# Order of the first and fourth unit, and the engine of some copies, in a two-layer transformer kernel

## The chip, the cores and the metric

The kernel runs on one core of a Trainium2 chip. A core has a matrix engine (TensorE, PE in the profile), a vector engine (VectorE, DVE), a scalar engine (ScalarE, ACT), a general engine (GpSimd, POOL) and SyncE (SP), which here only issues DMA transfers. Each engine works through its own queue in order and waits at semaphores for the others. Matmul results land in PSUM, everything else is in SBUF. The metric is the device time of one execution in microseconds (us); before the change the median of three runs is 738.88 us (738.88 to 739.01).

## The reference

The input `x` has four sequences (b) of 256 rows and 256 columns. Two layers follow each other, each an attention and a feed-forward part, each added to `x` after a layer norm. All is float32.

```python
def attn0(x):                              # 16 query heads, 8 key/value heads of 128
    q = einsum('btd,ndh->btnh', x, q_kernel); k, v = einsum('bsd,ckdh->cbskh', x, kv_kernel)
    q = apply_rope(rms_norm(q, q_norm_scale)); k = apply_rope(rms_norm(k, k_norm_scale))
    p = softmax(where((j <= i) & (i - j < 128), q @ k.T * 0.0884, -big))
    return einsum('btnh,nhd->btd', p @ v, out_kernel)
def ffn0(x):                               # keeps the 2 largest of each 4 columns of h
    h = silu(x @ w_gate) * (x @ w_up)
    return sparsify_2to4(h) @ w_down
def attn1(x):                              # 16 heads, causal, no rotation
    return softmax(causal(x @ W_Q @ (x @ W_K).T) * 0.0884) @ (x @ W_V) @ W_O
def ffn1(x):                               # fwht: Walsh-Hadamard transform of 1024 columns
    return fwht(silu(x @ W1.T) * (x @ W3.T)) @ W2.T
x = x + attn0(norm(x)); x = x + ffn0(norm(x)); x = x + attn1(norm(x)); x = x + ffn1(norm(x))
```

The lines are shortened: heads are written as matrix products. `rms_norm` divides each head's row by the root of its mean square; `apply_rope` turns its first and second half against each other by an angle that grows with the row.

## The kernel before

**Units.** Each attention is cut into 16 units. In attention 0 unit `n` is sequence `b` and head group `g` with `b, g = divmod(n, 4)`: 4 query heads and 2 key/value heads. A sequence's 256 rows are two blocks `t` of 128. Units go through a pipeline of stages (`pipelined`, lines 299 to 311): in step `s` stage `k` works on unit `s - lags[k]`, and the stages of one step are written in the sequence `order`. `behind` holds work that is written after a step.

**Stages of attention 0.** `project` (line 329, `project0`) multiplies the normed rows by the weights of 4 query heads, and by those of 2 keys and 2 values, block by block (matmul at line 443 into a bank `pj`). VectorE multiplies each result by a cosine and a sine table (line 448, `qc` and `qs`), ScalarE squares it (line 453, `sq`) and copies the values (line 455). `rotate` (`rotate0`, line 458) adds `qc` to `qs` with its halves exchanged (line 466, 768 columns: 6 heads), sums the squares of each head (line 467, `ss`), and on GpSimd makes the factors `r`, one over a root (lines 480, 483 and the power at 486, for 12 columns at once), with which it scales the keys (line 489). `turn` (`turn0`, line 495) transposes queries and keys: for units 0 to 5 and 14, 15 on TensorE (lines 504 and 515), with copies out of PSUM by VectorE (505) and ScalarE (516); for the rest the queries go over GpSimd (475) and a transposing DMA (477). `score` (`probabilities`, line 201) has score matmuls (213, 214), VectorE's masked maxima (216) and `nb` (223), ScalarE's exponentials (226), the reciprocal `rs` (231, VectorE) and GpSimd's scaling by it (234). `split` (`planes`, line 242) sorts each probability's two 16-bit halves apart on GpSimd (240) and sends them through a transposing DMA (249). `join` (`joined`, line 252) puts the turned halves together again (260), in attention 0 by ScalarE for both heads of a pair `kk`. `attend` multiplies with the values (391, 395). `out` multiplies by the output weights (292).

**Banks.** The results `pj` and the turned queries of the TensorE path share four PSUM slots (`half`); scores, turned keys of the TensorE path and `av` share four others (`bank`). A tile that gets a slot waits until the tile four before it has been read.

**Attention 1** has the same plan with stages `project`, `score` and `attend` (lines 691 to 726); products are formed by seven block products in place of eight (`seven_products`), whose last sums and copies are known as `last_of["sum"]` and `last_of["copy"]`. Its `joined` gives the first head of each pair to ScalarE and the second to VectorE.

**What sets the order.** The sequence within an engine's queue is made when the program is built, by a planner that takes the instructions in the order written but lets a later one pass where, by its modelled costs, an earlier one isn't ready. `tc.issue_after(x)` keeps the instructions of a block behind `x` on `x`'s engine. In the trace, for instance, unit 0's sum of block 0 (line 466) stands at 13.48 us, before the key products of block 1 (line 448) at 14.36. SyncE's transfers are issued as written: x of sequence 0, the identity, `wq` group 0, the tables, `wkv` group 0, x of sequence 1, then the rest.

Of the kernel before, what the change touches and what calls it, by code (L numbers as in the profile page):

```python
# [48 lines left out]
def two_layers(ctx, tc, consts, tables, x, wq, wkv, wo, w_gate, w_up, w_down,  # L49
# [49 lines left out]
    def attn_weight(name):  # L99
        return apool.tile([P, 4, NC, 512], F32, name=name)  # L100

    def load_group(t, src, g):
        nc.sync.dma_start(t[:, g], src[:, g])
# [8 lines left out]
    load_x(0)  # L112
    nc.sync.dma_start(cst[:, C_ID:C_HAD], consts[:, C_ID:C_HAD])
    wq_sb, wkv_sb = attn_weight("wq"), attn_weight("wkv")
    load_group(wq_sb, wq, 0)
    nc.sync.dma_start(tab, tables)
    load_group(wkv_sb, wkv, 0)
    load_x(1)
    nc.sync.dma_start(cst[:, C_HAD:], consts[:, C_HAD:])
    for g in range(1, 4):  # L120
# [193 lines left out]
    def attention0():  # L314
        with tc.tile_pool(name="attn0", bufs=2, reuse_waits="tile", side="right") as own:
# [22 lines left out]

            def rotated(n, held):
                rot, v = held  # L340
                rot, qT_planes, r = rotate0(rot, n >= 6, last_of["mx"] if 2 <= n < 14 else None)
                return rot, qT_planes, v, r

            def rotate(n, held):
                return rotated(n, held) if n < 14 else held

            def turn(n, held):
                rot, qT_planes, v, r = held
# [20 lines left out]
            def join(n, held):  # L369
                ps, v = held  # L370
                return [
                    joined(ps[kk], ((nc.scalar.copy, slice(0, 2), last_of["exp"]),))
                    for kk in range(2)
                ], v

# [26 lines left out]
            def out(b, t, gs, kept=False):  # L402
# [15 lines left out]
            behind[17] = [lambda _: xn_f.append(normed(0))]  # L418
            behind[19] = [lambda _: xn_f.append(normed(1)), *(out(3, t, (2, 3)) for t in range(NT))]
            pipelined(  # L420
                (project, rotate, turn, score, split, join, attend), (0, 0, 1, 2, 3, 4, 4),
                behind, (0, 5, 4, 3, 1, 2, 6),
            )

    def project0(own, xnT, g, cos_s, sin_s, first):


        v = own.tile([P, NT, 2, HD], F32, tag="v", name="v", bufs=5)
        rot = [
            [own.tile([P, 6, HD], F32, tag=tag, name=tag, bufs=n)  # L430
             for tag, n in (("qc", 4), ("qs", 2), ("sq", 2))] for _ in range(NT)
        ]

        queries, rest = (wq_sb, slice(0, 4)), (wkv_sb, slice(4, 6))
        parts = [(t, *part) for t in range(NT) for part in (queries, rest)]
        if first:
            parts = [(t, *part) for part in (queries, rest) for t in range(NT)]
        for t, w, hs in parts:
            qc, qs, sq = rot[t]
            pj = half([4, HD], "pj")  # L440
            n = hs.stop - hs.start
            for c in range(NC):
                last_of[0] = nc.tensor.matmul(  # L443
                    pj, lhsT=xnT[:, c, t * P : (t + 1) * P], rhs=w[:, g, c, :],
                    start=(c == 0), stop=(c == NC - 1),
                )
            for rot_to, tab in ((qs, sin_s), (qc, cos_s)):
                last_of["qc"] = nc.vector.tensor_tensor(  # L448
                    rot_to[:, hs], pj[:, 0:n],
                    tab[:, t, hs.start // 4, :].unsqueeze(1).to_broadcast([P, n, HD]),  # L450
                    ALU.mult,
                )
            nc.scalar.activation(sq[:, hs], pj[:, 0:n], AF.Square)  # L453
            if n == 2:
                last_of["v", t] = nc.scalar.copy(v[:, t, :, :], pj[:, 2:4])
        return rot, v

    def rotate0(rot, by_dma, first):

        r = small.tile([P, NT, 6], F32, tag="r", name="r")  # L460
        ss = small.tile([P, NT, 6], F32, tag="ss", name="ss")
        for t, (qc, qs, sq) in enumerate(rot):

            parts = [i.rearrange("p n (s h) -> p n s h", s=2) for i in (qc, qs)]
            with tc.issue_after(first.ins) if first else nullcontext():
                nc.vector.tensor_tensor(parts[0], parts[0], parts[1][:, :, ::-1, :], ALU.add)
            nc.vector.tensor_reduce(ss[:, t, :], sq, AX.X, ALU.add)
            rot[t] = qc
        qT_planes = None
        if by_dma:  # L470

            planes = page_of_planes([P, NT, 2, 4 * HD], "qpl")
            for t, qc in enumerate(rot):
# [1 line left out]
                copy_gpsimd(planes[:, t], words.rearrange("p (n w) -> p w n", w=2))  # L475
            qT_planes = page_of_planes([P, NT * 2 * 4, P], "qplT")
            nc.sync.dma_start_transpose(qT_planes, planes.rearrange("p t w n -> p (t w n)"))

        ve = small.tile([P, NT, 6], F32, tag="ve", name="ve")
        nc.gpsimd.tensor_scalar(  # L480
            ve[:, :, 0:4], ss[:, :, 0:4], 1.0, HD * RMS_EPS, ALU.mult, ALU.add
        )
        nc.gpsimd.tensor_scalar(
            ve[:, :, 4:6], ss[:, :, 4:6], 1.0 / HD, RMS_EPS, ALU.mult, ALU.add
        )
        nc.gpsimd.tensor_tensor(r.rearrange("p t h -> p (t h)"), ve.rearrange("p t h -> p (t h)"),
                                mhalf, ALU.pow)
        for t, qc in enumerate(rot):
            last_of["k"] = nc.gpsimd.tensor_tensor(
                qc[:, 4:6, :], qc[:, 4:6, :],  # L490
                r[:, t, 4:6].unsqueeze(2).to_broadcast([P, 2, HD]), ALU.mult,
            )
        return rot, qT_planes, r

    def turn0(own, rot, qT_planes, bank_of_k):
# [192 lines left out]
    def attention1(finish_ffn0):  # L688
# [23 lines left out]
        def attend(n, held):  # L712
# [3 lines left out]
            zTs[n] = zT = page("zT1")  # L716
            for kk in range(2):
                pT = joined(ps[kk], (
                    (nc.scalar.copy, slice(0, 1), last_of["copy"]),
                    (nc.vector.tensor_copy, slice(1, 2), last_of["sum"]),  # L720
                ))
                av = bank([2, T], "av1")
# [269 lines left out]
```

## Time and profile before

| | |
|---|---|
| Median of 3 runs | 738.88 us |
| The profiled execution | 737.64 us |
| Its span | 735.9 us |
| TensorE busy | 725.6 us (99%) |
| VectorE busy | 465.2 us (63%) |
| ScalarE busy | 412.2 us (56%) |
| GpSimd busy | 347.9 us (47%) |
| Granted TensorE clock | 1.00 in the span |

The profile is of one execution; its span runs from the first to the last instruction of the core, and what lies around the span makes up the rest of its time. Engine rows are shares of the span. "PEld" is TensorE's loading of weights, which overlaps its matmuls. Each float32 matmul of the program stands in the trace as two instructions. Attention 0 lasts to about 270 us, the first feed-forward part to about 375, attention 1 to about 645, the second feed-forward part to the end; they overlap at their seams.

### The profile page before, as it was taken

The numbers are of one execution on the slowest core, as the hardware profiler recorded it, in microseconds if no ns is written. First come the engines' busy times: TensorE is split into PE (matmuls) and PEld (weight loads), VectorE is DVE, ScalarE is ACT, GpSimd is POOL, SyncE is SP. The second block draws the span as 40 slices with busy tenths as digits, with TensorE's granted clock in tenths as the row PEclk, the third lists the DMA queues.
The fourth block names the chain that finished last, engine by engine and source line by source line (L and its number), as shares of the span: only waits on it lengthen the run. The fifth ranks groups of instructions, "written<-read, shape, count | busy, mean of one in ns | idle before, by whom it ended". The sixth has DMA issues, their size and how long they took to land.

```text
span 735.9 us, 11600 instructions
## 1 busy us (share of the span) xinstructions
PE 725.6 (99%) x3912; PEld 595.1 (81%) x3912; DVE 465.2 (63%) x1398; ACT 412.2 (56%) x987; POOL 347.9 (47%) x489
## 2 busy tenths in 40 slices
PE   9999999999999999999999999999999999999998
PEld 5556576666666778888898999999998999899997
DVE  6999878888887517977655644464442755464443
ACT  2487887667767962322356555555556576434332
POOL 1588978897799821011125433343336575520000
PEclk9999999999999999999999999999999999999999
DMA  8732354425446444001224432342232223401100
GB/s 333 289 65 53 56 93 81 92 52 94 89 76 101 86 121 166 16 14 45 99 72 86 126 48 44 77 124 44 44 73 44 44 44 44 91 12 22 24 13 30
DMA packets 138348, 57.51 MB, mean 78 GB/s; under 512 B 131504, under 2 KB 133680, under 8 KB 137520
## 3 DMA queue, kind: packets, MB, share of 16 engines
q1 hardware_dynamic: 138288, 56.77, 33.7%
q8 instruction: 31, 0.51, 0.3%
q14 instruction: 29, 0.24, 0.1%
HBM read 22.94 MB, written 1.05 MB: 33 GB/s over the span
## 4 chain that ended last, share of the span: by engine, by line
PE 73%; DVE 9%; POOL 7%; ACT 4%; issue 4%; DMA 2%; SPq 0%; POOLq 0%; ACTq 0%; DVEq 0%
PE pj L443 10%; PE pgu L547 8%; PE po_f L592 7%; PE po L292 7%; PE qk_x L777 5%; PE po L280 5%; PE sc L214 5%; PE gu_x L852 4%; PE av L391 3%; PE qk_y L777 3%; PE v_x L783 3%; PE av L268 2%; PE sc L213 2%; POOL p L234 2%; PE gu_y L852 2%
## 5 line engine op out<-in xcount | busy, mean ns | idle before, releaser
L234 POOL TENSOR_SCALAR p<-p,rs 128x128 f32<-128x128 f32 (+1 forms) x256 | 114.2, 464 | 149.9 <-DVE rs L231 144.6
L240 POOL TENSOR_SCALAR pl<-p 128x1536 uint16<-128x1536 uint16 x64 | 96.6, 1510 | 4.3
L260 ACT COPY pT<-plT 128x1536 uint16<-128x1536 uint16 (+1 forms) x64 | 92.0, 1493 | 11.6 <-DMA plT<-pl 11.6
L216 DVE CUSTOM_DVE_ANT_0 p<-sc,cst 128x128 f32<-128x128 f32 (+1 forms) x256 | 79.8, 352 | 10.4 <-PE sc L214 7.8
L226 ACT ACTIVATE p<-p,nb,r 128x128 f32<-128x128 f32 (+1 forms) x128 | 68.2, 534 | 18.8 <-DVE nb L223 18.7
L443 PE MATMUL pj<-wq,xnT 128*128 128x512 f32 x128 | 61.1, 595 | 1.1 <-DVE qT L505 1.1
L443 PE MATMUL pj<-wkv,xnT 128*128 128x512 f32 x128 | 60.1, 592 | 0.0
L292 PE MATMUL po<-wo,zT 128*128 128x256 f32 x256 | 57.9, 379 | 0.0
L226 ACT ACTIVATE p<-p,nb 128x128 f32<-128x128 f32 (+1 forms) x128 | 56.3, 447 | 2.8 <-DVE nb L221 2.8
L280 PE MATMUL po<-w_o,zT 128*128 128x256 f32 x256 | 57.6, 379 | 0.0
L453 ACT ACTIVATE sq<-pj 128x512 f32<-128x512 f32 (+1 forms) x64 | 31.0, 491 | 42.6 <-DVE qc L448 42.2
L292 PEld LDWEIGHTS po<-wo,zT 128*128 128x128 f32 x256 | 48.3, 190 | 7.0 <-ACT kT L516 0.6
L280 PEld LDWEIGHTS po<-w_o,zT 128*128 128x128 f32 x256 | 47.7, 190 | 6.0
L156 POOL TENSOR_SCALAR ve<-mv 128x2 f32<-128x2 f32 (+1 forms) x17 | 3.7, 220 | 98.1 <-DVE mv L152 97.6
L443 PEld LDWEIGHTS pj<-wkv,xnT 128*128 128x128 f32 x128 | 24.3, 190 | 30.2 <-issue 28.5
L448 DVE TENSOR_TENSOR qs<-pj,sin_s 128x512 f32<-128x512 f32 (+1 forms) x64 | 35.3, 552 | 13.4 <-PE pj L443 12.9
L443 PEld LDWEIGHTS pj<-wq,xnT 128*128 128x128 f32 x128 | 23.5, 190 | 24.2 <-issue 20.1
L663 ACT COPY qk<-qk_x 128x512 f32<-128x512 f32 x16 | 9.4, 587 | 57.6 <-PE qk_x L777 53.0
L268 PE MATMUL av<-pT,v 128*128 128x256 f32 x128 | 38.5, 383 | 1.0 <-ACT pT L260 0.9
L214 PE MATMUL sc<-kT,qT 128*128 128x256 f32 x128 | 38.3, 381 | 0.0
L214 PE MATMUL sc<-qk 128*128 128x256 f32 x128 | 38.2, 380 | 0.0
L240 POOL TENSOR_SCALAR qpl<-qc 128x1024 uint16<-128x1024 uint16 x20 | 29.2, 1474 | 18.0 <-PE av L395 8.2
(151 smaller groups left out, 1747.8 us busy)
## 6 DMA issues: line engine op xcount, KB each, us to landing
w<-in_w_dram SPq DMA_DIRECT2D x3, 1024.0 KB, 4.7
wq<-in_wq_dram SPq DMA_DIRECT2D x4, 512.0 KB, 7.6
wkv<-in_wkv_dram SPq DMA_DIRECT2D x4, 512.0 KB, 8.2
wo<-in_wo_dram SPq DMA_DIRECT2D x4, 512.0 KB, 10.2
w_qk<-in_w_q_dram SPq DMA_DIRECT2D x4, 512.0 KB, 4.8
w_qk<-in_w_k_dram SPq DMA_DIRECT2D x4, 512.0 KB, 5.8
w_v<-in_w_v_dram SPq DMA_DIRECT2D x4, 512.0 KB, 7.1
w_o<-in_w_o_dram SPq DMA_DIRECT2D x4, 512.0 KB, 6.1
```

The source lines that it names most:

```text
L214: nc.tensor.matmul(sc[:, P : 3 * P], lhsT=q[:, P:T], rhs=k, start=True, stop=True)
L216: last_of["mx"] = nc.vector.tensor_tensor_reduce(out=p[:, j, cols], in0=sc[:, cols], in1=mask[:, cols], scale=1.0, scalar=-3.0e38, op0=ALU ...
L226: last_of["exp"] = nc.scalar.activation(p[:, j, cols], p[:, j, cols], AF.Exp, bias=nb[:, j, i : i + 1], scale=SCALE1 if rq is None else rq ...
L234: nc.gpsimd.tensor_scalar(p[:, j, cols], p[:, j, cols], rs[:, j, i : i + 1], 1.0, ALU.mult, ALU.mult)
L240: last_of["planes"] = nc.gpsimd.tensor_scalar(o, i, 1.0, 1.0, ALU.mult, ALU.mult)
L260: copy(words.rearrange("p (n w) -> p w n", w=2), halves[:, :, js].rearrange("p w j n -> p w (j n)"),)
L268: nc.tensor.matmul(av, lhsT=v0, rhs=pT[:, 0:T], start=True, stop=False, skip_group_check=True)
L280: nc.tensor.matmul(po[:, t, :], lhsT=zT[:, j, t * P : (t + 1) * P], rhs=w[:, j, :], start=(t == j == 0), stop=(j == 3), skip_group_check=True,
L292: nc.tensor.matmul(po, lhsT=zTs[hd // 4][:, hd % 4, t * P : (t + 1) * P], rhs=w[:, hd, :], start=(hd == 0), stop=(hd == n - 1),)
L443: last_of[0] = nc.tensor.matmul(pj, lhsT=xnT[:, c, t * P : (t + 1) * P], rhs=w[:, g, c, :], start=(c == 0), stop=(c == NC - 1),)
L547: nc.tensor.matmul(o[:, j, :], lhsT=w[:, c, f0 + j, :], rhs=xnT[:, c, :], start=(c == 0), stop=(c == NC - 1),)
L777: last_of[1] = nc.tensor.matmul(o[:, j, :], lhsT=wqk[i - 1][:, j // 2, j % 2, :], rhs=x[i - 1], start=(first and j == 0), stop=True, skip_ ...
```

## The change

There are four edits.

1. The transfers of `wkv` group 0 and `wq` group 0 swap places. Unit 0 projects keys and values of both blocks first and then the queries of both. Its rotation is done apart: sums, squares' sums and factors of the two keys first, their scaling, and then the same for the four queries. Powers are taken per block there (two of 2 columns and two of 4) in place of one of 12. For the other units the same instructions are issued as before, now from the helpers `factors0` and `scaled`.
2. The rotation of unit 3 moves from the stage before `turn` of unit 2 in that step to a new stage `rotate_late` right behind it.
3. In attention 0 VectorE, not ScalarE, joins the second pair (`kk == 1`) of units 14 and 15.
4. In attention 1 VectorE, not ScalarE, joins the first head of both pairs of unit 0, without the constraint to stand behind a product's copy; the second head was VectorE's already.

```diff
     wq_sb, wkv_sb = attn_weight("wq"), attn_weight("wkv")
+    load_group(wkv_sb, wkv, 0)
+    nc.sync.dma_start(tab, tables)
     load_group(wq_sb, wq, 0)
-    nc.sync.dma_start(tab, tables)
-    load_group(wkv_sb, wkv, 0)
     load_x(1)
...
             def rotate(n, held):
-                return rotated(n, held) if n < 14 else held
+                return rotated(n, held) if n != 3 and n < 14 else held
+
+            def rotate_late(n, held):
+                return rotated(n, held) if n == 3 else held
...
                 return [
-                    joined(ps[kk], ((nc.scalar.copy, slice(0, 2), last_of["exp"]),))
+                    joined(ps[kk], ((
+                        nc.vector.tensor_copy if kk == 1 and n >= 14 else nc.scalar.copy,
+                        slice(0, 2), last_of["exp"],
+                    ),))
                     for kk in range(2)
...
             pipelined(
-                (project, rotate, turn, score, split, join, attend), (0, 0, 1, 2, 3, 4, 4),
-                behind, (0, 5, 4, 3, 1, 2, 6),
+                (project, rotate, turn, rotate_late, score, split, join, attend),
+                (0, 0, 1, 0, 2, 3, 4, 4),
+                behind, (0, 6, 5, 4, 1, 2, 3, 7),
             )
...
         if first:
-            parts = [(t, *part) for part in (queries, rest) for t in range(NT)]
+            parts = [(t, *part) for part in (rest, queries) for t in range(NT)]
...
+    def factors0(r, ss, ve, hs):
+        for part, scale, eps in ((slice(0, 4), 1.0, HD * RMS_EPS), (slice(4, 6), 1.0 / HD, RMS_EPS)):
+            if hs.start <= part.start < hs.stop:
+                nc.gpsimd.tensor_scalar(
+                    ve[:, :, part], ss[:, :, part], scale, eps, ALU.mult, ALU.add
+                )
+        o, i = (
+            [a[:, t, hs] for t in range(NT)] if hs.stop - hs.start < 6 else
+            [a.rearrange("p t h -> p (t h)")] for a in (r, ve)
+        )
+        for o_t, i_t in zip(o, i):
+            nc.gpsimd.tensor_tensor(o_t, i_t, mhalf[:, 0 : o_t.shape[-1]], ALU.pow)
...
-    def rotate0(rot, by_dma, first):
+    def rotate0(rot, by_dma, first, apart):
...
+        for hs in (slice(4, 6), slice(0, 4)) if apart else (slice(0, 6),):
+            for t, (qc, qs, sq) in enumerate(rot):
+                parts = [i[:, hs].rearrange("p n (s h) -> p n s h", s=2) for i in (qc, qs)]
+                with tc.issue_after(first.ins) if first else nullcontext():
+                    nc.vector.tensor_tensor(
+                        parts[0], parts[0], parts[1][:, :, ::-1, :], ALU.add
+                    )
+                nc.vector.tensor_reduce(ss[:, t, hs], sq[:, hs], AX.X, ALU.add)
+            if apart:
+                factors0(r, ss, ve, hs)
+                if hs.start == 4:
+                    scaled([qc for qc, _, _ in rot], r)
...
+        if not apart:
+            factors0(r, ss, ve, slice(0, 6))
+            scaled(rot, r)
         return rot, qT_planes, r
...
                 pT = joined(ps[kk], (
-                    (nc.scalar.copy, slice(0, 1), last_of["copy"]),
+                    (
+                        (nc.vector.tensor_copy, slice(0, 1), None) if n < 1 else
+                        (nc.scalar.copy, slice(0, 1), last_of["copy"])
+                    ),
                     (nc.vector.tensor_copy, slice(1, 2), last_of["sum"]),
                 ))
```

## The prediction

> **What bounds the kernel now.** I read the page's busy row first, then TensorE's waits, then the timelines around the places where it waits. The page says:
>
> ```profile
> span 735.9 us, 11600 instructions
> PE 725.6 (99%) x3912; PEld 595.1 (81%) x3912; DVE 465.2 (63%) x1398; ACT 412.2 (56%) x987; POOL 347.9 (47%) x489
> ```
>
> TensorE works nearly all the time, and the change leaves its matmuls as they are. So all that can be won is idle time of TensorE: 735.9 - 725.6 = 10.3 us, with 1.2 us before its first matmul and about 3 us after its last. The list of its waits (total, times, longest) names who ends them:
>
> ```profile
> PE tr_k L515 <- POOL qc L489: 1.6, 2, 1.2
> PE pj L443 <- DVE qT L505: 1.1, 2, 0.9
> PE av L391 <- DVE mx L216: 1.0, 2, 0.8
> PE av L268 <- ACT pT L260: 0.9, 2, 0.7
> ```
>
> The timeline of TensorE places them (start, duration, and in brackets the idle time before):
>
> ```profile
> 22.14 0.44 PE L515 MATMUL tr_k<-cst,qc 128*128 128x128 f32 x2 [1.22 <-POOL qc L489]
> ...
> 50.09 1.98 PE L443 MATMUL pj<-wq,xnT 128*128 128x512 f32 x4 [0.91 <-DVE qT L505]
> ...
> 72.05 1.13 PE L391 MATMUL av<-pT,v 128*128 128x512 f32 x2 [0.83 <-DVE mx L216]
> ...
> 399.02 0.70 PE L268 MATMUL av<-pT,v 128*128 128x256 f32 x2 [0.68 <-ACT pT L260]
> ```
>
> Matmul ends are modelled, so I count from start to start: a 128x128 matmul normally gives way to the next after 0.22 us with its pair, and by that count the four places cost about 1.38, 1.07, 0.99 and 0.84 us. The first two and the last are where three of the edits work. But the share of VectorE by stretch shows a second bound at the beginning:
>
> ```profile
> core 0: us, PE busy (x) PEld busy (x) DVE busy (x) ACT busy (x) POOL busy (x), PEclk, DMA share, GB/s
> 30.00:40.00 10.00, 9.80 (x46) 6.28 (x45) 9.86 (x33) 6.52 (x22) 6.05 (x9) 1.00 0.13 53
> 40.00:50.00 10.00, 9.17 (x41) 5.70 (x39) 9.90 (x32) 7.65 (x25) 6.86 (x11) 1.00 0.43 79
> 60.00:70.00 10.00, 10.00 (x37) 5.87 (x37) 9.93 (x26) 9.02 (x20) 8.99 (x14) 1.00 0.42 78
> 90.00:100.00 10.00, 10.00 (x35) 6.07 (x34) 6.10 (x12) 7.77 (x16) 8.93 (x14) 1.00 0.51 94
> ```
>
> VectorE is full from 10 to about 72 us and has room only after 78. Between 10 and 72 us a hole closed in TensorE is worth only what VectorE then finishes sooner, since the wait at 72.05 is for VectorE's maxima. VectorE's own idle time there is small:
>
> ```profile
> 28.42 0.69 DVE L448 TENSOR_TENSOR qs<-pj,sin_s 128x512 f32<-128x512 f32 x1 [0.45 <-PE pj L443]
> 30.14 0.42 DVE L448 TENSOR_TENSOR qs<-pj,sin_s 128x256 f32<-128x256 f32 x1 [0.43 <-PE pj L443]
> ```
>
> From 100 to 230 us TensorE goes through its units at 15.96 us each with GpSimd idle 2 us in most, so what is ahead at 78 us stays ahead.
>
> **The change, part by part.**
>
> *First unit's keys first and apart.* The two weight loads swap places on SyncE's queue; both are 512 KB, landing at 5.99 and 9.05 us, and the part projected first needs its weights at 6.49, the second at 10.02. Either order fits: 0. The tables and both x loads keep their places behind the same bytes. The keys' products are then with VectorE from 10.3 us on, and their sums can end between 13.0 us (right behind the four 0.33 us products) and about 15.5 us (behind the queries' products too). GpSimd then needs one 0.20 us factor step, two powers of two columns (0.70 us each by the L157 row of that size) and two scalings at 0.61: 2.9 us with issue, so keys stand at 16 to 19 us, before TensorE turns them at 20.8. The queries' two powers of four columns, by interpolation between 0.70 us (2 columns) and 2.27 (12), are 1.0 us each; they end by 21.5, and nobody needs them before the first `nb` at 34.58. So the hole of 1.38 closes. What is late next: two projection banks of unit 2 wait for the copies of the turned queries (VectorE, 24.83), and VectorE is full. It gains its two pauses, 0.53 + 0.50 = 1.03 us from start to start, and pays for splitting two sums and two reductions: 768 columns take 0.86 us from start to start, 256 take 0.33 and 512 take 0.60, so 0.93 - 0.86 = 0.07, four times: 0.28. The scalings now fall near VectorE's own L466 sums. A collision costs VectorE from 0 to two times 0.61; I take 0.2. Part: -1.03 + 0.28 + 0.2 = -0.55, rounded **-0.6**.
>
> *Fourth unit's sums behind the third's turn.* The two copies (1.2 us) pass ahead of two sums and two reductions (3.5 us), so the bank of the matmul at 50.09 comes free before it is wanted at 49.0: 1.07 us closes. But VectorE has the same work, and reaches unit 4's products at 50.5 as before. It saves only pauses behind TensorE near 53.8 and 55.9, with their rounding about 0.35. Behind TensorE's gained time the next wait is the fourth unit's keys: L489 began at 56.08 and `tr_k` at 56.74 already followed on its heels, after GpSimd had worked without a pause since 47.68. That start hangs on `rs` (L231, 47.42) in VectorE's queue between the very sums that move. It moves by -0.4 to +3.0 us. TensorE stood 0.83 us at 72.05, which is its spare for this. I take no effect of it, and 0.35 from VectorE: **-0.35**.
>
> *Who meets whom.* In this stretch VectorE lost time to GpSimd:
>
> ```profile
> 57.53 1.98 DVE L466 TENSOR_TENSOR qc<-qc,qs 128x768 f32<-128x768 f32 x1
> 57.23 1.47 POOL L240 TENSOR_SCALAR pl<-p 128x1536 uint16<-128x1536 uint16 x1
> 70.60 1.06 DVE L223 SCALAR_TENSOR_TENSOR nb<-mx,r 128x4 f32<-128x4 f32 x1
> 70.17 1.47 POOL L240 TENSOR_SCALAR pl<-p 128x1536 uint16<-128x1536 uint16 x1
> ```
>
> The sum takes 0.95 and `nb` 0.16 elsewhere; both ended here just behind the GpSimd copy. With those at 44.03 and 56.11 such losses are 3.1 us. The edits shift the two engines against each other, so they are dealt anew: at best TensorE's whole 0.93 at 72.05 goes, at worst it grows by as much. I take 0, and +-0.9 for the range.
>
> *VectorE at the end of attention 0* (second pair of units 14 and 15). TensorE has no hole there: 253 to 362 us is solid, with `av` of unit 15's second pair issued at 268.73 and ScalarE's copy done at 268.2. VectorE's copy would take about 1.0 us (a 128x1024 one takes 0.68, a 128x768 one 0.59) in place of 1.92, but it starts with the transfer's landing, and it may push GpSimd's work at 258.3 by up to 1.0. The holes at 250.8 and 252.7 belong to unit 13, which the edit leaves alone: **0**. Were that cover gone, ScalarE's 0.95 would be its worth.
>
> *VectorE at the start of attention 1* (unit 0, first head of each pair). For the second pair ScalarE copies at 397.93, behind four exponentials; the data landed at 394.30. On VectorE, idle from 396.64 to 398.06, the copy ends at 397.2; TensorE would ask at 398.18. The 0.84 hole closes. For the first pair it is open. ScalarE finished at 395.60 and TensorE lost 0.31 there. The data landed at 391.14, but VectorE's queue was full to 395.49. The row of these copies is 0.59 us, and if one fits in before 393 the 0.31 goes too, with 0.1 of restart: -1.25. The Trainium skill speaks against that: "SBUF — State Buffer", section "Who interferes with whom", says that a VectorE copy in a two-port mode and a GpSimd instruction exclude each other, and whichever comes second waits for the first to end. GpSimd's L240 runs from 393.62 to 395.09, so a copy put there would end no earlier than 395.6, and with both heads in one queue at 396.0: +0.4, so -0.44 for the part. This trace has both kinds: one copy at 592 ns beside no GpSimd work, another at 1053 under it. I take the middle, **-0.85**. The maxima behind such a copy feed unit 1's exponentials up to 1 us later; its pair is joined at 406.6 and later, having landed at 405.18, so with some cover.
>
> Sum: -0.6 - 0.35 + 0 + 0 - 0.85 = **-1.8 us**. The profiled execution took 737.64 (span 735.9 and 1.7 around it): 735.8 expected. The runs' median is 738.88, 1.2 above it, and I carry the difference over: **737.1**.
>
> **The rivals.**
> - *Both seams and the collisions too.* The new phase frees 0.93 at 72.05, and the first pair's copy fits early (-0.4 more): -1.8 - 1.3 = -3.1, 735.8. For it: the losses are chance meetings of 0.6 to 1.5 us instructions. Against: GpSimd is 90% busy from 60 us on, so others wait.
> - *VectorE keeps the early gain.* The start gives nothing because VectorE is full and has four more instructions; only attention 1 pays: 738.0 to 738.4. For it: 9.9 of 10 us busy. Against: the two pauses at 28 and 30 us.
> - *Slower: `rs` gets behind all the sums.* If the planner sets unit 1's `rs` behind two copies and four sums, it comes at 45.7 + 1.2 + 3.5 = 50.4 in place of 47.42. GpSimd's unbroken run to L489 starts 3.0 later, unit 3's keys come 3.0 later, TensorE has 0.83 of spare: +2.2, and with the later meetings of GpSimd and VectorE at worst +3.1. Less 0.6 of the first part and 0.85 at attention 1: +1.65, 740.5. Without such meetings it passes 0.2% (1.48 us) only from 1.48 + 0.6 + 0.85 + 0.83 = 3.8 us of lateness, with the worst of them from 2.9. Against: `rs` stood between the sums before.
>
> **How the numbers follow.** Main case 0.46 (own range 736.3 to 737.9), collisions freed 0.20, early gain kept by VectorE 0.21, slower 0.13. What a measurement can tell from no change is about 0.2%, 1.48 us: the line is 737.4. The main case lies on its fast side for two thirds (0.31), so faster 0.31 + 0.20 = 0.51; same 0.15 + 0.21 = 0.36; slower 0.13. The range goes down to 735.3 (the second case's edge) and up to 739.9, which takes in the slower case's beginning and leaves out some 0.1.
>
> **What would show it.** Right: no wait before `tr_k` at 20.8; no pause of VectorE at 28 and 30; unit 4's second query projection at once behind its keys; the wait for the maxima near 71 still there; the wait at 399 gone; 15.96 us per unit as before. Wrong: GpSimd's run near 47 starting late, a longer wait of `tr_k` near 56, VectorE's sums of 1.5 us and more before 31 us, or new holes of TensorE after 100 us, where I expect the order unchanged.

## The result and the profile after

| | before | after |
|---|---|---|
| Median beside each other, 6 runs each | 738.94 us | 741.21 us |
| Ratio, 95% interval | | 1.0034 (1.0024 to 1.0044) |
| The profiled execution | 737.64 us | 741.07 us |
| Its span | 735.9 us | 739.2 us |

The change makes the kernel slower by 2.3 us, above the 0.2% that a measurement here can tell. The page of the changed kernel has nearly the same busy rows as before; TensorE has 0.9 us more and the span 3.3 us:

```profile
span 739.2 us, 11599 instructions
PE 726.5 (98%) x3912; PEld 595.6 (81%) x3912; DVE 472.6 (64%) x1406; ACT 406.5 (55%) x983; POOL 347.5 (47%) x492
```

So most of the loss is idle time of TensorE. Its waits (in total, times, longest; rows left out are marked) have changed hands:

```profile
PE tr_k L541 <- POOL qc L483: 2.3, 3, 1.5
PE av L397 <- DVE mx L216: 1.3, 2, 0.8
PE tr_n L182 <- DVE xn L171: 1.3, 2, 0.8
...
PE av L268 <- DVE nb L221: 1.1, 1, 1.1
...
PE pj L450 <- DVE qT L531: 0.5, 2, 0.3
```

The wait for copies of turned queries (1.1 before) is down to 0.5, as meant. New is the third row: the transposes of a normed sequence wait for its normalisation. The timeline of TensorE has the places (start, duration, line, in brackets the idle time before):

```profile
57.34 0.44 PE L541 MATMUL tr_k<-cst,qc 128*128 128x128 f32 x2 [1.51 <-POOL qc L483]
...
84.30 0.44 PE L182 MATMUL tr_n<-cst,xn 128*128 128x128 f32 x2 [0.47 <-DVE xn L171]
...
85.77 0.44 PE L182 MATMUL tr_n<-cst,xn 128*128 128x128 f32 x2 [0.81 <-DVE xn L171]
...
219.07 1.12 PE L397 MATMUL av<-pT,v 128*128 128x512 f32 x2 [0.52 <-DVE mx L216]
...
246.20 1.10 PE L397 MATMUL av<-pT,v 128*128 128x512 f32 x2 [0.80 <-DVE mx L216]
...
399.30 0.70 PE L268 MATMUL av<-pT,v 128*128 128x256 f32 x2 [1.07 <-DVE nb L221]
```

To see where the span grows, I took the start of the same matmul in both traces and subtracted (after minus before):

| Matmul | before at, us | offset, us |
|---|---|---|
| unit 2's projection, first block | 23.07 | -0.56 |
| unit 2's projection, second block | 26.50 | +0.03 |
| unit 4's projection, second block | 50.09 | -0.91 |
| unit 0's `av` | 57.67 | +1.23 |
| unit 6's projection | 74.73 | +0.13 |
| unit 7's projection | 82.71 | 0.00 |
| unit 7's projection, second block | 96.14 | +1.40 |
| unit 10's `av` | 217.07 | +2.01 |
| unit 15's `av` | 267.44 | +2.64 |
| attention 1, unit 1's scores | 385.66 | +2.95 |
| attention 1, unit 2's scores | 405.94 | +2.93 |
| last feed-forward part, first `gu_x` | 654.61 | +3.34 |

Edits 1 and 2 act before 60 us, and by 82.71 their gains and losses have cancelled to nothing. Edit 4 acts at 395 to 400, and the offset on both sides of it is the same. Nearly all of the 3.3 us arises at 84 us (+1.4), 219 and 246 us (+0.6 each) and 365 us (+0.3), where no line is edited; another 0.4 comes after 600. As much, 0.3 to 0.5, stands in every trace of a kernel with the split keys (also in those of only_a and a_c_d below, not in that of keys_in_one), so it goes with edit 1; why is open.

### The profile page after: what moved, and what is told of

The parts are those of the page before. It is cut to its first block, busy times and chain, and to the rows that moved or that the text cites. A ratio compares the mean times of both kernels' runs of the same rounds, so it can differ in the third digit from the quotient of the medians.

```text
span 739.2 us, 11599 instructions
## 1 busy us (share of the span) xinstructions
PE 726.5 (98%) x3912; PEld 595.6 (81%) x3912; DVE 472.6 (64%) x1406; ACT 406.5 (55%) x983; POOL 347.5 (47%) x492
## 4 chain that ended last, share of the span: by engine, by line
PE 75%; POOL 9%; DVE 7%; issue 4%; ACT 3%; DMA 2%; SPq 0%; POOLq 0%; ACTq 0%; DVEq 0%
PE pj L450 9%; PE pgu L573 7%; PE po_f L618 7%; PE po L292 7%; PE qk_x L806 6%; PE po L280 5%; PE sc L214 5%; PE gu_x L881 4%; POOL p L234 3%; PE av L397 3%; PE qk_y L806 3%; PE v_x L812 3%; PE sc L213 2%; PE av L268 2%; POOL pl L240 2%
## 5 line engine op out<-in xcount | busy, mean ns | idle before, releaser
L234 POOL TENSOR_SCALAR p<-p,rs 128x128 f32<-128x128 f32 (+1 forms) x256 | 116.7, 475 | 152.3 <-DVE rs L231 146.7
L240 POOL TENSOR_SCALAR pl<-p 128x1536 uint16<-128x1536 uint16 x64 | 94.3, 1474 | 4.8 <-POOL p L234 0.5
L260 ACT COPY pT<-plT 128x1536 uint16<-128x1536 uint16 (+1 forms) x60 | 86.2, 1494 | 11.7 <-DMA plT<-pl 11.7
```

The source lines that it names most:

```text
L234: nc.gpsimd.tensor_scalar(p[:, j, cols], p[:, j, cols], rs[:, j, i : i + 1], 1.0, ALU.mult, ALU.mult)
L240: last_of["planes"] = nc.gpsimd.tensor_scalar(o, i, 1.0, 1.0, ALU.mult, ALU.mult)
L260: copy(words.rearrange("p (n w) -> p w n", w=2), halves[:, :, js].rearrange("p w j n -> p w (j n)"),)
```

## The experiments

Two theories stood at the start. **P**: the edits themselves cost little; the moved sums change the order of the queues and the phase of VectorE against GpSimd further down, and instructions meet there that did not meet before. **D**: the edits cost where they stand, by more and shorter instructions on a full VectorE and by collisions there. Edits 1 to 4 are called (a) to (d) here. A run's figure is a median; the kernel before was run beside each group: 737.84 us beside the first four kernels, 738.84 beside the next four, 738.80 beside the third four and 738.86 beside the last three. Compare within a group. The expectations of the first four were written for a kernel before at 738.9, so there only differences count. The edits are shown shortened.

### Each edit alone, and all but (b)

```diff
 only_a:  first unit: wkv first, (rest, queries), apart          (b), (c), (d) as before
 only_b:  (project, rotate, turn, rotate_late, score, ...)       (a), (c), (d) as before
 only_d:  joined(...): nc.vector.tensor_copy if n < 1            (a), (b), (c) as before
 a_c_d:   the changed kernel with the stages of before
```

> Edit (a) alone on the kernel before. Theory P (the loss is made by the queue orders that the moved sums of unit 3 set off, and by meetings of VectorE and GpSimd further down): GpSimd's queue after unit 0 stays as before, so only the start's own +0.2 us is left by unit 2, the tr_n matmuls at 84 us wait as before, and the time is 738.7 to 739.7. Theory D (the edits cost where they stand: more and shorter VectorE instructions at the start): the start carries a good part of the +2.3 us, 739.9 or more. The prediction's own step said -0.6: 738.3.

Measured: 738.54 against 737.84, ratio 1.0007 (0.9999 to 1.0015). The offsets are those of the changed kernel at the start: -1.03 at unit 0's key transposes, -0.60 at unit 2's projection, -0.01 at its second block, +0.03 at unit 7's. The difference of +0.7 fits P. The gain was returned at two waits which the kernel before does not have:

```profile
22.47 1.98 PE L446 MATMUL pj<-wq,xnT 128*128 128x512 f32 x4 [0.27 <-ACT sq L456]
...
26.49 0.70 PE L446 MATMUL pj<-wq,xnT 128*128 128x512 f32 x1 [0.33 <-DVE qT L527]
```

From start to start they cost 0.43 and 0.49 us. (a) gives nothing at the start; the prediction's -0.6 is not there.

> Edit (b) alone on the kernel before. Theory P: the four scalings of unit 3's second pair stand ahead of unit 5's key factors in GpSimd's queue, the two normalisations of sequence 2 at about 83 us take over 2 us together where they took 0.73, the first transposes of that sequence wait some 1.3 us more, and the time is +1.3 to +2.6: 740.2 to 741.5. Theory D: the move itself costs what its collisions at 45 to 60 us cost, which the spare at 72 us swallows: 738.6 to 739.3. The prediction's own step said -0.35: 738.6.

Measured: 738.93, ratio 1.0017 (1.001 to 1.0024), 1.1 more: just under P's 1.3 to 2.6, and more than D's 0.4 at most. The two normalisations took 2.12 us in its trace (2.25 in the changed kernel's). Its profiled execution, at 741.12 the slowest of its 18, showed one thing more. After the waits of 1.47 and 0.41 us at 57 the granted clock fell (stretches of 2 us, PE, PEld, DVE, ACT, POOL; the last three columns are clock, DMA share, GB/s):

```profile
57.00:59.00 2.00, 1.38 (x9) 1.14 (x10) 2.00 (x4) 1.31 (x5) 2.00 (x3) 0.90 0.00 0
59.00:61.00 2.00, 2.00 (x4) 0.94 (x4) 1.11 (x3) 2.00 (x9) 1.39 (x2) 0.50 0.03 8
61.00:63.00 2.00, 2.00 (x6) 1.23 (x5) 1.76 (x4) 2.00 (x8) 1.91 (x5) 0.75 1.22 196
63.00:65.00 2.00, 2.00 (x6) 0.97 (x6) 0.73 (x3) 2.00 (x3) 2.00 (x3) 1.00 0.07 5
```

> Edit (d) alone on the kernel before (VectorE joins both pairs of the first unit of the second attention). Theory P: everything up to 390 us is as before; the wait that the join shortens is taken over by the wait of the first av for VectorE's nb, so 0 within 0.3: 738.6 to 739.2. The prediction's own step said -0.85: 738.1.

Measured: 737.80, ratio 1.0000 (0.9992 to 1.0009). Theory P's number, but the wait is not for `nb`, as these timelines of VectorE, GpSimd and TensorE show:

```profile
393.70 0.57 DVE L260 COPY pT<-plT 128x768 uint16<-128x768 uint16 x1
...
396.14 1.43 DVE L650 TENSOR_TENSOR xs<-xnT,xs 128x128 f32<-128x128 f32 x1
397.49 0.41 DVE L216 CUSTOM_DVE_ANT_0 p<-sc,cst 128x256 f32<-128x256 f32 x1
...
397.83 0.58 DVE L260 COPY pT<-plT 128x768 uint16<-128x768 uint16 x1
398.32 0.15 DVE L221 TENSOR_SCALAR nb<-mx 128x4 f32<-128x4 f32 x1
398.38 1.07 DVE L260 COPY pT<-plT 128x768 uint16<-128x768 uint16 x2
...
395.96 1.47 POOL L240 TENSOR_SCALAR pl<-p 128x1536 uint16<-128x1536 uint16 x1
...
394.82 0.59 PE L268 MATMUL av<-pT,v 128*128 128x256 f32 x2
...
396.80 0.61 PE L802 MATMUL qk_y<-xs,t_qk 128*128 128x128 f32 x4
398.48 0.70 PE L268 MATMUL av<-pT,v 128*128 128x256 f32 x2 [1.07 <-DVE nb L221]
```

This trace runs 2.1 us late here (1.0 from a later start, 1.2 from the meeting at 212 us below), and the comparisons take that off. The moved copy of the first pair, for its first head, is the one at 393.70: only that pair's data had landed by then (at 393.26, the second pair's at 396.41). It fitted in early, and ended 3.5 us sooner than ScalarE's copy in the kernel before (395.60). But the planner then gave TensorE another order: the first head's `av` (394.82) went ahead of products that stood in front of it before, and the second head's (398.48) ahead of half of `qk_y` and of `v_zy`. TensorE so asked for the second head 1.1 us sooner than before, and waited for that head's copy, which was VectorE's already: it ends at 398.41 (the releaser named is the instruction that ended closest by), 0.2 later than before. It stands behind a combination of 1.43 us, whose like takes 0.29 in the median and which ended here 0.14 behind GpSimd's plane copy; the kernel before has the same 1.43. What the second pair gained the first lost.

> The changed kernel with edit (b) undone. Theory P: the queue order of GpSimd at 80 us is that of before and the wait there is gone; what stays are the start's +0.2 and at most one of the +0.6 meetings: 738.6 to 739.8. Theory D: without (b) nearly all of the loss stays, +1.5 to +2.5: 740.4 to 741.4.

Measured: 738.44, ratio 1.0005 (0.9998 to 1.0012). Without (b) the offset at 96 us is -0.08, and D falls: 0.6 us of loss is left.

### What happens at 84 us

Here is the kernel before, VectorE and then GpSimd:

```profile
83.47 0.73 DVE L171 TENSOR_SCALAR xn<-x,mv,rstd 128x256 f32<-128x256 f32 x2
...
82.94 0.61 POOL L489 TENSOR_TENSOR qc<-qc,r 128x256 f32<-128x256 f32 x1
83.64 0.28 POOL L156 TENSOR_SCALAR ve<-mv 128x2 f32<-128x2 f32 x1
84.01 0.75 POOL L157 TENSOR_TENSOR rstd<-ve,mhalf 128x2 f32<-128x2 f32 x1
84.75 1.47 POOL L240 TENSOR_SCALAR pl<-p 128x1536 uint16<-128x1536 uint16 x1
```

And the changed one:

```profile
83.47 2.25 DVE L171 TENSOR_SCALAR xn<-x,mv,rstd 128x256 f32<-128x256 f32 x2
...
82.91 1.19 POOL L483 TENSOR_TENSOR qc<-qc,r 128x256 f32<-128x256 f32 x2
84.06 1.51 POOL L240 TENSOR_SCALAR pl<-p 128x1536 uint16<-128x1536 uint16 x1
85.65 0.19 POOL L156 TENSOR_SCALAR ve<-mv 128x2 f32<-128x2 f32 x1
```

The normalisations start at the same 83.47 in both. In the changed kernel each ends 0.15 behind a GpSimd instruction, the second key scaling and the plane copy; one by one they took 0.77 and 1.55 us, where both took 0.40 before. In GpSimd's queue unit 3's four scalings of probabilities stand ahead of unit 5's key factors now, and the plane copy ahead of the statistics of lines 156 and 157. Of the four edits (b) alone changes the queue there (only_b's trace has the changed order, those of only_a, only_d and a_c_d that of before); VectorE's reductions of unit 5 moved with it.

```diff
 order_back, on the changed kernel: scalings of unit 3's second pair kept back
+            for fn in between[:1 - t]:          # in scaled(), unit 5, behind key scaling 0
+                with tc.issue_after(key.ins):
+                    fn()                        # the four p <- p * rs
```

> The changed kernel with unit 3's four scalings of the second pair put back between unit 5's two key scalings on GpSimd; nothing else of the order of any engine but GpSimd changes. Theory P: the two normalisations of sequence 2 no longer meet the key scaling and the 1.47 us plane copy, so 0.9 to 1.3 less than the changed kernel. Rival (the reductions of unit 5, which (b) moved behind unit 3's maxima on VectorE, make the chain late whatever GpSimd's order is): within 0.3 of the changed kernel.

Measured: 740.99; the changed kernel in the same group 740.96. The rival's number: putting the scalings back is not enough:

```profile
83.04 2.27 DVE L171 TENSOR_SCALAR xn<-x,mv,rstd 128x256 f32<-128x256 f32 x2
...
83.07 0.61 POOL L493 TENSOR_TENSOR qc<-qc,r 128x256 f32<-128x256 f32 x1
83.66 1.50 POOL L245 TENSOR_SCALAR pl<-p 128x1536 uint16<-128x1536 uint16 x1
```

The second key scaling runs at 83.07 to 83.68, within 0.13 of its time in the kernel before, so this chain isn't late, as the rival would have it. What the order has not restored is the two short instructions between scaling and copy. They are put there by hand next:

```diff
 spacer, on the changed kernel: in planes(), unit 3, second pair
+            apart = small.tile([P, 2], F32, ...)
+            with tc.issue_after(last_of["k"].ins):
+                after = nc.gpsimd.tensor_scalar(apart, mhalf[:, 0:2], 0.0, 1.0, ALU.mult, ALU.add)
+            with tc.issue_after(after.ins):
+                after = nc.gpsimd.tensor_tensor(apart, apart, mhalf[:, 0:2], ALU.pow)
+        with tc.issue_after(after.ins) if after else nullcontext():
             copy_gpsimd(s, ...)
```

> The changed kernel with two GpSimd instructions of 2 columns (a scale and a power on a tile of their own, what lines 156 and 157 do) between unit 5's second key scaling and the 1.5 us plane copy at 84 us: in the kernel before, lines 156 and 157 stand at that place, in the changed one the copy follows the key scaling at once. Theory P2 (putting the four scalings back did nothing because the copy still followed the key scaling at once and took the port before the second normalisation): the second normalisation takes 0.4 in place of 1.55 us, the transposes of sequence 2 wait 0.3 to 0.6 in place of 1.6 us, and the time is 0.7 to 1.2 less than the changed kernel. Rival: the normalisations themselves come too late: within 0.3 of the changed kernel.

Measured: 739.88 beside 738.80, ratio 1.0011 (1.0003 to 1.0019). The changed kernel stood 2.1 above its own neighbour, this one 1.1: 1.0 less, P2's number. The 0.98 us (start to start) in front of the second transposes are gone, the 0.65 in front of the first stay:

```profile
83.80 1.12 DVE L171 TENSOR_SCALAR xn<-x,mv,rstd 128x256 f32<-128x256 f32 x2
...
84.42 0.23 POOL L251 TENSOR_SCALAR apart<-mhalf 128x2 f32<-128x2 f32 x1
84.74 0.74 POOL L255 TENSOR_TENSOR apart<-apart,mhalf 128x2 f32<-128x2 f32 x1
85.47 1.47 POOL L240 TENSOR_SCALAR pl<-p 128x1536 uint16<-128x1536 uint16 x1
```

### The meeting at 212 us

Around 219 and 246 us the order of all queues is the same in both kernels. In the kernel before, VectorE and GpSimd have

```profile
210.63 0.96 DVE L466 TENSOR_TENSOR qc<-qc,qs 128x768 f32<-128x768 f32 x1
214.50 1.31 DVE L466 TENSOR_TENSOR qc<-qc,qs 128x768 f32<-128x768 f32 x1
...
210.64 3.09 POOL L486 TENSOR_TENSOR r<-ve,mhalf 128x12 f32<-128x12 f32 x1
214.97 2.17 POOL L240 TENSOR_SCALAR pl<-p 128x1536 uint16<-128x1536 uint16 x1
```

and in the changed one

```profile
212.03 1.02 DVE L498 TENSOR_TENSOR qc<-qc,qs 128x768 f32<-128x768 f32 x1
215.90 1.91 DVE L498 TENSOR_TENSOR qc<-qc,qs 128x768 f32<-128x768 f32 x1
...
212.02 2.28 POOL L478 TENSOR_TENSOR r<-ve,mhalf 128x12 f32<-128x12 f32 x1
215.54 1.48 POOL L240 TENSOR_SCALAR pl<-p 128x1536 uint16<-128x1536 uint16 x1
```

Before, the sum is up to 10 ns ahead of the power and the power takes 3.09 us; after, it is 10 ns behind, and the power takes 2.28. GpSimd is thereby 0.8 us sooner at its plane copy, starts it ahead of the second sum and not behind it, and that sum takes 1.91 in place of 1.31. All maxima behind it come 0.6 us later, and `av` waits for them. At 246 us it is `nb`, ahead of other maxima, that meets a plane copy. First the kernel before, then the changed one:

```profile
242.60 0.43 DVE L223 SCALAR_TENSOR_TENSOR nb<-mx,r 128x4 f32<-128x4 f32 x1
241.54 1.47 POOL L240 TENSOR_SCALAR pl<-p 128x1536 uint16<-128x1536 uint16 x1
...
244.67 1.04 DVE L223 SCALAR_TENSOR_TENSOR nb<-mx,r 128x4 f32<-128x4 f32 x1
244.23 1.47 POOL L240 TENSOR_SCALAR pl<-p 128x1536 uint16<-128x1536 uint16 x1
```

`nb` takes 0.16 elsewhere and ends within 0.02 of the copy's end here, both times. The changed kernel's GpSimd is by then at its next copy, and `nb` meets it nearer to its beginning. A faster GpSimd makes a slower kernel. The traces of only_a, only_b and only_d show the power first and the two waits too. In that of a_c_d both start at 210.56, the power takes 3.10, and neither wait is there. only_d has up to there exactly the queues of the kernel before.

```diff
 gp_touch, on the changed kernel, unit 13, ahead of the power
+            nc.gpsimd.tensor_scalar(ve[:, :, 4:6], ve[:, :, 4:6], 1.0, 0.0, ALU.mult, ALU.add)
 dve_touch, on the kernel before, unit 14, block 0, ahead of the sum
+                nc.vector.tensor_scalar_mul(qs[:, 5, 0:1], qs[:, 5, 0:1], 1.0)
```

> The changed kernel once more, beside runs of the kernel before and of the next three on the same chip. Theory P: +1.4 by 100 us of the span in every execution, and +1.2 more wherever GpSimd's power of unit 13 starts ahead of VectorE's sum of unit 14 at about 212 us; +2.3 to +3.2 in the median. Some executions show a granted clock under 1 from the hole that (b) makes at 57 us (the three of six before were +0.7). If the meeting at 212 us falls either way from execution to execution, the spans fall into two groups 1.2 us apart.

Measured: 740.96 beside 738.84, ratio 1.0027 (1.0016 to 1.0037). The power came first in its trace too. Its executions did not fall into two groups.

> The changed kernel with one more GpSimd instruction of 4 columns right before unit 13's power at 212.0 us (it multiplies two columns by 1.0). Theory P (the meeting there decides which of two instructions takes the longer time, and the rest follows): the power starts some 0.2 us behind the sum, takes 3.1 in place of 2.3 us, the plane copy at 215.5 comes behind the second sum, the waits at 219 and 246 us fall back to 0.07 and 0.35, and the time is 1.2 less than the changed kernel, although GpSimd has more to do. Rival (the waits of 219 and 246 us come from VectorE's or ScalarE's own work): no change, or +0.2.

Measured: 739.73, 1.2 less than the changed kernel in the same group, P's number, with one instruction more:

```profile
212.03 0.98 DVE L502 TENSOR_TENSOR qc<-qc,qs 128x768 f32<-128x768 f32 x1
...
212.01 0.20 POOL L474 TENSOR_SCALAR ve<-ve 128x4 f32<-128x4 f32 x1
212.29 2.85 POOL L482 TENSOR_TENSOR r<-ve,mhalf 128x12 f32<-128x12 f32 x1
```

The `av` waits fell to 0.09 and 0.32 us from start to start.

> The kernel before with one more VectorE instruction of one column right ahead of unit 14's first sum at 210.6 us (it multiplies one column by 1.0). Theory P: the power now starts first in every execution, takes 2.3 us, and the waits at 217 and 243 us grow by 0.6 each: +1.2 over before, 739.0 where before is 737.8. Rival: +0.1, what the instruction itself takes.

Measured: 738.75 against 738.84, no change: P's +1.2 did not come. But in its trace the power came first (210.31, the sum at 210.39, 2.27 us), and the waits at 217 and 244 us had grown to 0.66 and 0.94. Both can hold if the kernel before itself had the power first in most executions of this group. Its spans fit that: above 736.6 us there were 14 of 54 beside the first four kernels, and 31 of 32, 46 of 51 and 41 of 43 in the later groups, with medians of 736.1 and then 737.0 to 737.1. It fits also that the run of the prediction's profile was 1.2 us below the median, and that the traced executions of keys_in_one and only_c, with the power held up to 3.10 and 3.09 us, are the fastest of their 22 and 13, 1.4 and 0.9 below the median, while only_d's, with the power first, is the slowest of its 13, 1.9 above. Only one of the kernel before's executions has a trace, so for the others it is argued.

### Edit (d) by halves, edit (a) without the split, and a better kernel

```diff
 second_pair, on the kernel before
-                    (nc.scalar.copy, slice(0, 1), last_of["copy"]),
+                    (nc.vector.tensor_copy, slice(0, 1), None) if n < 1 and kk == 1 else
+                    (nc.scalar.copy, slice(0, 1), last_of["copy"]),
 keys_in_one, on the kernel before: wkv first and (rest, queries), rotate0 not apart
 touch_and_pair: second_pair and the GpSimd instruction of gp_touch, on the kernel before
```

> The kernel before with the second pair alone of the second attention's first unit joined by VectorE (ScalarE keeps the first pair's first head). Theory P (with both pairs on VectorE the first pair's join stands behind the 1.4 us combination of line 628/650 and the maxima there, and what the second pair gains is lost by the first): the first pair's wait stays 0.3 us, the second's falls from 0.84 us to 0.1 or less, 0.7 to 0.9 less than before. Rival (VectorE is the bound there whatever is joined): within 0.2 of before.

Measured: 737.90 against 738.80, ratio 0.9984 (0.9977 to 0.9990). P's number: the first pair waits 0.31 us from start to start, the second not at all. P's reason does not hold: as only_d's trace shows, the first pair's moved copy does not stand behind the combination. What second_pair leaves as it was is the first pair's copy on ScalarE and TensorE's order around its `av`.

> The kernel before with edit (a)'s order alone (the key and value products of unit 0 and their transfer first), sums, factors and scalings of unit 0 in one piece as before. If splitting is what spends the gain of (a) on VectorE: the hole ahead of unit 0's key transposes stays about as before (1.0 to 1.4 us), the waits of 0.3 us at 22.5 and 26.5 us of the span do not appear, and by unit 2's second half the offset is -0.3 to +0.3, the time within 0.4 of before. If the order is what costs: both of those waits are there, and the time is 0.5 or more above before.

Measured: 738.90 against 738.80, ratio 0.9998 (0.9991 to 1.0004). In its trace unit 0's key transposes still wait, 0.90 us from start to start, and unit 2's first projection waits 0.47 for ScalarE's squares, while the wait at 26.5 is absent. So the split brings the wait at 26.5, but the one at 22.5 comes with the order. With the split or without it, the order gives nothing at the start.

> The kernel before with the second pair joined by VectorE and with one GpSimd instruction of 4 columns ahead of unit 13's power, so that the sum of unit 14 starts first in every execution. Theory P: what second_pair gives, and 1.2 less in those executions where the power came first in the kernel before: 0.7 to 2.1 less than before, and hardly any execution in the slower group. Rival: no better than second_pair.

Measured: 736.62 against 738.80, ratio 0.9963 (0.9949 to 0.9977), the best of all kernels here: 2.2 less than before, where the changed one is 2.1 more, and all seven executions within 0.5 us.

### Do the causes add up?

```diff
 mended, on the changed kernel: spacer, gp_touch's instruction, and in (d)
-                        (nc.vector.tensor_copy, slice(0, 1), None) if n < 1 else
+                        (nc.vector.tensor_copy, slice(0, 1), None) if n < 1 and kk == 1 else
 only_c:     the kernel before with (c)
 without_c:  the changed kernel without (c)
```

> The changed kernel with three things at once: the two short GpSimd instructions of spacer, the one of gp_touch, and edit (d) cut down to the second pair. If the three account for what the change lost and for what (d) missed, 1.1 + 1.2 + 0.9 = 3.2 less than the changed kernel, so about 1.0 below the kernel before where that is 738.8: 737.4 to 738.2. If something else of the four edits costs as well, or one of the three does not add up, 738.5 or more.

Measured: 737.57 against 738.86, ratio 0.9987 (0.9980 to 0.9993), so 1.3 us below the kernel before, where the changed kernel stood 2.1 above it in its own group: 3.4 together where 3.2 were expected. In its one trace the power came a whole microsecond behind the sum and the wait at 244 us was there nevertheless; with a span of 736.8 it is the slowest of its 17 executions at full clock, whose median is 735.7. The instruction shifts the odds at that place; it is no guarantee.

> Edit (c) alone on the kernel before (VectorE joins the second pair of units 14 and 15). The prediction's own step and theory P both say 0: within 0.3 of before. If (c) is behind the 0.3 us that the changed kernel loses at 365 us, the last h of the first feed-forward part starts 0.46 us behind the end of its last matmul, not 0.10, and the wait of qk_x grows from 0.44 to 0.75 us.

Measured: 738.78, ratio 1.0001 (0.9993 to 1.0009), with `h` released as before.

> The changed kernel with edit (c) undone. If (c) together with (b) makes the 0.3 us at 365 us: 0.3 less than the changed kernel, and h there starts 0.10 us behind its matmul. Otherwise as the changed kernel, 2.1 above before.

Measured: 740.49, ratio 1.0024 (1.0017 to 1.0032); 0.5 less than the changed kernel had in another group. In its trace the wait at 365 us is back to 0.43 us and the last `h` starts 0.10 us behind its matmul, where it was 0.46 in every trace with (b) and (c) together. (c) alone doesn't do it, (a), (c) and (d) together don't, and without (c) it is absent. So these 0.3 us belong to (c) beside (b), with (a) in every such kernel too, which no run separates. Why that `h` is released later, with the same matmuls ahead of it, stays open.

## Why the prediction was wrong

The step that weighs most is the fourth unit's: put at -0.35, it cost 1.1, because it changed GpSimd's order at 84 us.

**The first unit (-0.6).** Closing the hole of 1.38 was right. The failed term is what comes next, "-1.03 + 0.28 + 0.2". VectorE's two pauses shrank to nothing and 0.2, nearly as said, but VectorE reached the copies of the turned queries 0.97 us later (25.80 for 24.83): 0.22 stood in the trace before its first product (10.56 for 10.34), and the same work in smaller pieces took 0.75 more, where the sum had put 0.28. And ScalarE's squares, which the sum did not have, held up unit 2's first projection. The part is +0.03 by unit 2's second block, and with the split keys another 0.3 to 0.5 is lost after 600 us. The rival "VectorE keeps the early gain" had the start right. The hole itself was one draw: in the seven traces with the same queues up to there, TensorE's idle time before `tr_k` is 0.75 to 1.85 us, and the prediction's profile had 1.22.

**The fourth unit (-0.35).** The hole at 50.09 closed. `rs`, on which the slower rival hung, was not late (47.32 for 47.42). But the four scalings behind it took 2.94 us in place of 2.25 and the key scalings 1.90 in place of 1.19, both beside VectorE's sums: GpSimd was 0.6 and then 1.3 us later, while TensorE, with the hole at 50 closed, asked 0.9 us sooner. So it waited 1.51 and 0.41 at 57. As the prediction said, the 0.83 us of spare at 72 took that up: net 0.0 at 82.71, so VectorE's -0.35 did not come either. What failed is "what is ahead at 78 us stays ahead": I took the queues behind the edited place as given. With (b) the planner gave GpSimd another order between 76 and 87 us, and the second normalisation met a 1.5 us copy. That is +1.1 in only_b's median where (b) was put at -0.35. From 100 to 250 us the order was unchanged, as expected; the holes at 219 and 246 came without a change of order.

**Who meets whom (0, +-0.9).** The mechanism was right; place and size were not. I had counted the meetings between 44 and 72 us only. Those at 84 us (1.2) and at 212 us (1.2 over the two waits that follow) are each larger than the whole term.

**VectorE at the end of attention 0 (0).** Right alone: ratio 1.0001. Beside (b) it costs 0.3 us.

**VectorE at the start of attention 1 (-0.85).** The second pair was right: -0.9 measured when alone. The step that failed is that the first pair hangs on when its moved copy fits in. That copy met the better end: it started at 393.70 in only_d's late trace, 391.6 in the time of the kernel before, well ahead of the 393 that was asked. The 0.31 were not won, because the sum took TensorE's order and the pair's second head as given. TensorE asked for that head 1.1 us sooner, its copy came 0.2 later, and the wait of 1.07 took the whole gain. The port rule was put at the wrong instruction: the first pair's moved copy was not held (0.57 us), but the combination ahead of the second head's copy was, 1.43 us, and in the kernel before as well.

**The base.** "I carry the difference over" treated 1.2 us between the profiled execution and the median as something lying around the span. More likely it is the meeting at 212 us, two outcomes of one kernel, and both traces of the changed kernel show the slower one. Part of the span's 3.3 us against the medians' 2.3 would be that.

The slower rival had the sign but not the cause, and the range's upper end was drawn from a cause that did not come.

## What to carry to other kernels

Where a planner orders the queues, cost an edit by the whole new order, not by the edited lines: compare the sequences of every engine, also far behind, before a sum of saved waits is believed. Look in the trace for pairs that start within some 20 ns of each other on VectorE and GpSimd, as at 212 us here; each can be a coin whose two sides are worth more than the edit, and one short instruction in front can make the better side likelier. When work moves from one engine to another, ask what the planner will put first once it is ready sooner, and what that will then wait for; an early copy alone won nothing here.

## What the runs showed of the hardware

**A meeting is not the same from both sides.** With VectorE's 128x768 sum starting level with GpSimd's power of 12 columns or up to 10 ns ahead of it, the power took 3.09 us, 0.8 more than alone (six traces: 3.09 to 3.10); with the power starting 10 to 20 ns ahead, both ran at nearly their own time, 2.28 and 1.02 (six further traces: 2.27 and 1.00). The Trainium skill, "SBUF — State Buffer", section "Who interferes with whom", lists a VectorE instruction with two SBUF inputs as one that contends with a GpSimd instruction that reads SBUF, and says that whoever issues first has the shared ports for the whole instruction and that the other blocks. The plane copy and the normalisation of 256 columns agree (1.55 us for 0.40); a power first does not hold up the sum. The measurement decides: for this power only one direction blocks. Who was first can't be read from starts this close: in the changed kernel the first normalisation at 84 us starts at 83.47, the second key scaling at 83.48, and yet the normalisation is the one that is held (0.77 for 0.40).

**The clock falls more often with (b).** In only_b's trace the granted clock was 0.50 in a whole stretch after the two waits at 57 us, and unit 5's projection came 1.6 us later than in the changed kernel's trace, which has the same two waits at a clock of 1.00. Over all executions with (b) a mean clock of 0.998 or less was seen in 27 of 103, in those without it in 4 of 303; in only_b such executions had a span of 738.1 us in the median, 1.0 above the others. That the waits at 57 bring it on is argued from that one trace. The hole of 1.85 us at 22 us in only_d and second_pair showed no such fall, so the length of one hole does not decide it; what does stays open.
